# A graph network's prologue: first loads shared by two queues, and the second layer's weights folded during the first norm

## The chip, the cores and the metric

The kernel runs on one core of a Trainium2 chip. A core has TensorE (PE: matrix products and 128x128 transposes into PSUM), VectorE (DVE), ScalarE (ACT), GpSimd (POOL) and SyncE (SP), which here only issues transfers. Each engine runs its own list of instructions in order, and waits on semaphores for the others. Transfers are issued by SP and by POOL; 16 DMA engines carry them out. The metric is the device time of one execution in microseconds (us). Before the change its median is 2506.15 us over 4 runs (2505.47 to 2507.16).

## The reference

There are B = 16 graphs of N = 1024 nodes with D = 128 features, each with a dense adjacency of 1024 x 1024, all in float32. Two blocks follow each other, each with a residual and a layer norm:

```python
# block 0: one GNN layer
degree = adj.sum(-1)[:, :, None]
agg = einsum('bid,bij->bjd', x, adj) / degree
x = layernorm(x + relu(concat([x, agg], -1) @ W.T + b))
# block 1: four layers; layers 2 and 3 take earlier outputs beside the last one
src = nodes @ ws + bs;  dst = nodes @ wd + bd;  own = nodes @ wn + bn
src_agg = einsum('bjv,bij->biv', src, adj / row_norm)      # l2 norms of rows
dst_agg = einsum('bjv,bji->biv', dst, adj / column_norm)   # and of columns
out = tanh(concat([src_agg, own, dst_agg]) @ wu + bu)
x = layernorm(x + four_layers(x))
```

The kernel folds wu into ws, wd and wn once ("fold"), so that a layer is one product with a folded weight (message weights wm), one with the own weight (wown) and the two aggregations.

## The kernel before, in words

**Tiling.** A graph's adjacency lies in SBUF as eight blocks of 128 rows x 1024 columns (tile a), its nodes as eight blocks of 128 x 128 (xn). "Half" 1 is the latter four blocks or the latter 512 columns, half 0 the first. Columns sums of squares and row sums of squares give the norms; the transposed adjacency (at) is made by VectorE from rows loaded a second time (load_rows, in quarters q = 0 to 3), scaled by the inverse row norms (scale_rows) and transposed in blocks (transpose_rows).

**Batches.** A loop over b runs the four layers of graph b. While it does, the loads, norms and first GNN of graph b + 1 are woven into the layers' steps by hooks: a dictionary from a step's number to a function. For graph 0 nothing can be woven in, so a prologue (lines 718 to 909) does its loads, its first GNN and its norm, and layer 0 of graph 0 is a plain one (plain_layer) with its own hooks. The order of instructions on PE, DVE, ACT and POOL is the order in which the code writes them (line 712); SP's transfers follow program order too, each waiting until the one eight before it on its queue has landed.

**The prologue, step by step.**

- SP and POOL load w0, x and adjacency. A "pair" is two blocks of adjacency, 1 MB; SP loads two of its four row groups, POOL the other two. PAIRS goes through half 1 first. Then come b0 and the weights of the four layers (fetch_weights, eight small DMAs a layer), into a raw buffer that is the second adjacency buffer; rows of quarter 2 follow layer 0's weights, those of quarter 3 layer 1's.
- make_identity writes the identity that transposes on PE need; it is on POOL.
- to_xT, with_x and weights_of_x transpose x of a half, put x in the accumulator of the residual (yn) and start the product with W (pw).
- squares_of takes squares (ACT) and degrees (DVE) of a pair; gathers_of multiplies it with xn into pa (PE); add_square sums squares on POOL, into what becomes the column norms.
- degree_inverses, degree_row and scaled divide pa by the degree (agT); weights_of_agT ends pw and applies the relu (yT); with_y adds y to the residual; norm_stats and norm_write (or norm_write_act on ACT) are the layer norm; to_x1 transposes its result.
- fold_begin and fold_end fold one layer's weights: transposes of ws, wd, wn and products with the biases, then the products with wu. fold_end writes the folded weights to DRAM (wsave), from which message_weights fetches them.

**Buffers that decide an order.** The small PSUM tiles come from a pool of two (`small`), the larger ones from a pool of four (`product` without a number). A new tile waits until the oldest one in its pool has been read.

Of the kernel before, what the change touches and what calls it, by code (L numbers as in the profile page):

```python
# [9 lines left out]
AF = mybir.ActivationFunctionType  # L10
ALU = mybir.AluOpType
# [3 lines left out]
P = 128  # L15
NL = 4
CHUNKS = [1, 1, 2, 3]
G = 4
# [5 lines left out]
def adj_resnorm_kernel(ctx: ExitStack, tc: tile.TileContext, x, adj, w0, b0, layers, out):  # L24
# [113 lines left out]
            wm = flat[:, :(nch + 1) * 2 * P].rearrange("p (c v) -> p c v", c=nch + 1)  # L138
        return wr, wur, bc, wm, [raw.take(3 * P).rearrange("p (k v) -> p k v", k=3) for _ in range(nch)]

    def fold_begin(l, fetched, copy=nc.scalar.copy):

        wr, wur, bc, wm, wTs = fetched
        for c in range(CHUNKS[l]):
            pt = small(f"wtr{l}_{c}", [BPH, P])
            for k in range(3):
                nc.tensor.transpose(pt[:, k], wr[:, k, c], ident)
            copy(wTs[c], pt[:, :3])
        pm = small(f"bm{l}", [HW])
        for k in range(2):  # L150
            nc.tensor.matmul(pm[:, k * P:(k + 1) * P], bc[:, k:k + 1].to_broadcast([P, P]),
                             wur[:, PART[k]], start=True, stop=True)
        nc.tensor.matmul(pm[:, 2 * P:2 * P + 1], wur[:, PART[2]], bc[:, 2:3], start=True, stop=True)
        nc.scalar.copy(wm[:, 0], pm[:, :2 * P])
        nc.scalar.activation(bout[l], pm[:, 2 * P:2 * P + 1], AF.Identity, bias=bc[:, 3:4])

    def fold_end(l, fetched):
        _, wur, _, wm, wTs = fetched
# [571 lines left out]
    def load_nodes(h, q=nc.sync):  # L730
        for g in range(G):
            q.dma_start(xn[g * C:(g + 1) * C, h * BPH:(h + 1) * BPH], xv[h][g])

    nc.sync.dma_start(w0n, w0)
    for p, pair in enumerate(PAIRS):
        if p % 2 == 0:
            load_nodes(1 - p // 2)
        load_pair(nc.sync, pair, range(G // 2))
        load_pair(nc.gpsimd, pair, range(G // 2, G))
    make_identity(nc, ident)  # L740
    nc.sync.dma_start(b0c, b0.rearrange("(p o) -> p o", o=1))
    raw = Raw()
    wm = message_tile("wm1_0")
# [19 lines left out]
    def to_xT(h):  # L763
        pt = small(f"xtr0_{h}", [HW])
        for q in range(BPH):
            nc.tensor.transpose(pt[:, q * P:(q + 1) * P], xn[:, h * BPH + q], ident)
        nc.scalar.copy(nodes(xT[:, half(h)]), blocks(pt))
# [6 lines left out]
    sq = []  # L774
# [10 lines left out]
    def square(i):  # L785
        nc.scalar.activation(sq[i], a[:, i, :], AF.Square, accum_out=cols[:, i:i + 1])

    def add_square(i):
        nc.gpsimd.tensor_add(sq[4], sq[4], sq[i])

    def degree(i):
        nc.vector.reduce_sum(cols[:, 2 * NB + i:2 * NB + i + 1], a[:, i, :], axis=AX.X)

    def degree_inverses(h):
        s = slice(2 * NB + h * BPH, 2 * NB + (h + 1) * BPH)
        nc.vector.reciprocal(inv[:, s], cols[:, s])

    def gather(h, i):
        nc.tensor.matmul(pa[h], xn[:, i], a[:, i, half(h)], start=(i == BPH), stop=(i == BPH - 1))  # L799
# [18 lines left out]
    def degree_row(h):  # L818
        nc.scalar.copy(nodes(dinv[:, half(h)]), blocks(factor_bank(2, h, inv, f"dinv0_{h}")))

    def scaled(h):
        nc.vector.tensor_mul(agT[:, half(h)], pa[h], dinv[:, half(h)])

    def weights_of_x(h):
        pw[h] = product(f"pw0_0_{h}")
        nc.tensor.matmul(pw[h], w0T[:, 0], xT[:, half(h)], start=True, stop=False)

    def weights_of_agT(h):
        nc.tensor.matmul(pw[h], w0T[:, 1], agT[:, half(h)], start=False, stop=True)
        nc.scalar.activation(blocks(yT[:, half(h)]), nodes(pw[h]), AF.Relu, bias=b0c)  # L830

    def with_x(h):

        pn[h] = ps_t.tile([P, BPH, P], F32, tag="pt", name=f"yn0_{h}")
        nc.tensor.matmul(pn[h].rearrange("p q d -> p (q d)"), ident, xn[:, h * BPH:(h + 1) * BPH].rearrange("p q d -> p (q d)"),
                         start=True, stop=False)
# [9 lines left out]
            nc.tensor.transpose(pt[:, q * P:(q + 1) * P], x1n[:, h * BPH + q], ident)  # L846
        nc.scalar.copy(x1T[:, half(h)], pt)
# [12 lines left out]
    weights_of_x(0)  # L860
    degree_inverses(1)
    degree_row(1)
    squares_of(*PAIRS[2])
# [1 line left out]
    add_square(0)  # L865
    add_square(1)
    first, second = 2, 3
    square(first)
    square(second)
    gather(1, first)  # L870
    gather(1, second)
    degree(first)
    degree(second)
    degree_inverses(0)
    degree_row(0)
    gather(0, first)
# [35 lines left out]
    for b in range(B):  # L912
# [306 lines left out]
```

## Time and profile before

| what | value |
|---|---|
| median of 4 runs | 2506.15 us |
| the profiled execution's own time | 2505.47 us |
| its span, first to last instruction | 2503.7 us |
| PE busy over the span | 2484.4 us |
| mean granted PE clock | 0.998 |
| first gather (pa) on PE | 12.10 us |
| first x1n of the norm on ACT | 36.49 us |
| first d product of layer 0 | 48.5 us |
| start of the load of graph 1's adjacency | 77.42 us |

Times in the trace count from the span's start. A float32 product appears as two passes (128x512: 0.43 us each at full clock), so sixteen passes are eight products. A pass's row in the list of instructions gives start and duration, and in brackets the idle time of its engine before it with what ended that; durations overlap, so for sums the distances from start to start, as the chain that ended last shows them, are used. "PEclk" is the share of full clock that PE was granted.

### The profile page before, as it was taken

The page shows a single profiled execution, that of the slowest core. Times are in us where ns is not written, and L with a number is a line of the kernel's source. Part 1 is how long each engine was busy: PE and PEld are TensorE (multiplying, and loading weights), DVE is VectorE, ACT ScalarE, POOL GpSimd, SP SyncE. Part 2 cuts the span into 40 slices and gives each one's busy share as a digit, 9 for nine tenths or more (in the row PEclk, how much of TensorE's full clock was granted, in tenths as well). Part 3 has the DMA queues.
Part 4 walks back from the last instruction along what each step waited for, and adds up shares of the span by engine and source line. Part 5 has one row for each costly group of instructions (what it writes and reads, how often), then busy time and mean ns, then how long its engine had stood idle before and what let it go on. Part 6 is the DMA issues. An engine that isn't in the chain of part 4 may idle for free.

```text
span 2503.7 us, 30302 instructions
## 1 busy us (share of the span) xinstructions
PE 2484.4 (99%) x11693; PEld 1059.8 (42%) x11693; DVE 1660.6 (66%) x2030; ACT 836.4 (33%) x1553; POOL 519.9 (21%) x217
## 2 busy tenths in 40 slices
PE   8999999999999999999999999999999999999998
PEld 4443344433444344453434434334443344433444
DVE  5858667585675757667576675766758567585643
ACT  5414333142331423324143241432414333142411
POOL 5401204112040121302113030130301203112000
PEclk9999999999999999999999999999999999999999
DMA  9417245271543715426163451634417254271410
GB/s 201 99 47 147 55 96 104 51 143 41 102 100 66 134 34 104 106 66 127 35 124 84 86 106 47 131 65 101 96 46 147 54 100 102 51 144 40 93 24 9
DMA packets 358735, 219.63 MB, mean 88 GB/s; under 512 B 148928, under 2 KB 329408, under 8 KB 358592
## 3 DMA queue, kind: packets, MB, share of 16 engines
q1 hardware_dynamic: 357184, 213.51, 42.0%
q0 software_dynamic: 1408, 4.20, 0.7%
q8 instruction: 92, 1.51, 0.3%
q14 instruction: 51, 0.42, 0.1%
HBM read 199.17 MB, written 18.46 MB: 87 GB/s over the span
## 4 chain that ended last, share of the span: by engine, by line
PE 89%; SPq 3%; DMA 3%; DVE 2%; issue 2%; ACT 2%; POOL 0%; POOLq 0%; DVEq 0%; ACTq 0%
PE m L691 35%; PE z L691 26%; PE pt L503 15%; PE pa L179 8%; SPq L231 2%; PE pw L179 2%; DMA a<-in_adj_dram 2%; DVE e L664 1%; DMA out_dram<-y 1%; PE pa L799 1%; PE d L554 1%; ACT sq L248 0%; ACT sq L245 0%; POOL acc L250 0%; DVE cols L247 0%
## 5 line engine op out<-in xcount | busy, mean ns | idle before, releaser
L378 POOL TENSOR_TENSOR rs<-ve,mhalf 128x32 f32<-128x32 f32 x30 | 162.8, 5427 | 1363.9 <-DVE ve L376 1363.9
L691 PE MATMUL m<-T,S 128*64 128x512 f32 x1008 | 395.9, 594 | 0.0
L691 PE MATMUL z<-at,t 128*64 128x512 f32 x1224 | 383.7, 592 | 0.0
L691 PE MATMUL m<-a,t 128*64 128x512 f32 x1008 | 366.7, 594 | 0.0
L691 PE MATMUL m<-Q,S 128*64 128x512 f32 x768 | 339.2, 593 | 0.0
L691 PE MATMUL m<-at,t 128*64 128x512 f32 x828 | 311.2, 592 | 0.0
L506 DVE TENSOR_TENSOR t<-pt,wm 128x512 f32<-128x512 f32 x256 | 175.4, 690 | 169.5 <-PE pt L503 169.4
L252 POOL TENSOR_TENSOR acc<-acc,sq 128x1024 f32<-128x1024 f32 x90 | 220.6, 2451 | 138.9 <-ACT sq L248 135.3
L691 PE MATMUL z<-a,S 128*64 128x512 f32 x504 | 228.3, 593 | 0.0
L691 PE MATMUL z<-T,t 128*64 128x512 f32 x504 | 226.8, 592 | 0.0
L691 PE MATMUL z<-a,t 128*64 128x512 f32 x504 | 226.8, 592 | 0.0
L336 DVE TENSOR_TENSOR a<-a,cinv 128x512 f32<-128x512 f32 x250 | 157.8, 700 | 96.1 <-DMA cinv<-dr 92.8
L457 ACT ACTIVATE a<-a,rinv 128x256 f32<-128x256 f32 x480 | 198.2, 495 | 55.1 <-DMA a<-in_adj_dram 45.1
L503 PE MATMUL pt<-wm,f1T 128*128 128x256 f32 x768 | 213.8, 384 | 0.1
L179 PE MATMUL pa<-a,xn 128*64 128x512 f32 x960 | 208.7, 592 | 0.0
L691 PE MATMUL z<-at,S 128*64 128x512 f32 x444 | 202.6, 593 | 0.0
L691 PEld LDWEIGHTS m<-Q,S 128*64 128x64 f32 x768 | 104.1, 137 | 208.0 <-issue 206.1
L591 ACT COPY e<-m 64x512 f32<-64x512 f32 x63 | 36.6, 581 | 447.4 <-PE m L691 447.1
L691 PEld LDWEIGHTS m<-T,S 128*64 128x64 f32 x1008 | 117.8, 137 | 159.8 <-issue 158.7
L691 PE MATMUL z<-Q,t 128*64 128x512 f32 x384 | 172.6, 592 | 0.0
L691 PEld LDWEIGHTS z<-at,t 128*64 128x64 f32 x1224 | 120.8, 137 | 120.4 <-issue 111.3
L691 PEld LDWEIGHTS m<-a,t 128*64 128x64 f32 x1008 | 110.0, 137 | 125.7 <-issue 120.1
(197 smaller groups left out, 3783.8 us busy)
## 6 DMA issues: line engine op xcount, KB each, us to landing
a<-in_adj_dram SPq DMA_DIRECT2D x120, 512.0 KB, 12.8
a<-in_adj_dram SPq DMA_DIRECT2D x480, 128.0 KB, 4.1
xn<-in_x_dram SPq DMA_DIRECT2D x128, 64.0 KB, 2.0
wm<-wsave SPq DMA_DIRECT2D x16, 512.0 KB, 3.9
wm<-wsave SPq DMA_DIRECT2D x31, 256.0 KB, 3.1
xs<-in_x_dram SPq DMA_DIRECT2D x60, 128.0 KB, 3.5
cinv<-dr SPq DMA_DIRECT2D x30, 256.0 KB, 5.2
dinv<-dr SPq DMA_DIRECT2D x30, 256.0 KB, 5.0
```

Of the source, the lines that this page charges most:

```text
L179: nc.tensor.matmul(out[s], x[:, s], y, start=start, stop=stop)
L231: nc.sync.dma_start(ov[g, :, ks], ys[g * C:(g + 1) * C, ks])
L252: nc.gpsimd.tensor_add(acc, acc, sq)
L336: engine.tensor_mul(a[:, i, s], a[:, i, s], cinv[:, s])
L378: nc.gpsimd.tensor_tensor(rstd, ve, mhalf[:, :n], ALU.pow)
L457: nc.scalar.activation(st[:, k], st[:, k], AF.Copy, scale=rinv[:, q * QB + k:q * QB + k + 1])
L503: nc.tensor.matmul(pt[:, q], f[:, i * P:(i + 1) * P], wm[:, 1 + c], start=(k == 0), stop=(k == nch - 1))
L506: nc.vector.tensor_add(t[j][:, o:o + 2].rearrange("p k a v c -> p k (a v c)"), pt, wm[:, 0][:, None, :].to_broadcast([P, 2, 2 * P]))
L554: nc.tensor.matmul(nodes(o) if len(y.shape) == 4 else o, x_, y, start=start, stop=stop)
L591: nc.scalar.copy(e0[high], A[high])
L664: nc.vector.tensor_add(e0[high], e0[high], e1[high])
L691: nc.tensor.matmul(o, x, y, start=start, stop=stop)
```

## The change

Five things change, all in the prologue and in layer 0 of graph 0.

- x of both halves is loaded ahead of all adjacency, and each of the two queues takes half of the row groups of x, as it does of adjacency. The identity is written after POOL's share of x and ahead of its adjacency.
- The x steps of both halves (to_xT, with_x, weights_of_x) stand ahead of all gathers.
- Layer 1's weights are loaded ahead of quarter 2's rows and layer 2's ahead of quarter 3's; quarters 0 and 1 go on SP after layer 3's weights instead of on POOL during the norm.
- The end of the first GNN is reordered: one of the degrees goes to ACT as a copy with a sum; half 1 is scaled and multiplied ahead of half 0's last gather; squares of blocks 2 and 3 come later; the row norms' inverse and the last add of squares stand after the statistics.
- Layer 1's weights are folded between the norm's steps, with one copy on DVE and its bias copies put off (biases), instead of by hooks of layer 0. The hooks move: the fold of layer 2 to steps 5 and 8, that of layer 3 to 9 and 12. The column sums' transpose goes from the norm to the messages (first_half0).

```diff
-    def fold_begin(l, fetched, copy=nc.scalar.copy):
+    def fold_begin(l, fetched, copy=nc.scalar.copy, later=False):
...
-        nc.scalar.copy(wm[:, 0], pm[:, :2 * P])
-        nc.scalar.activation(bout[l], pm[:, 2 * P:2 * P + 1], AF.Identity, bias=bc[:, 3:4])
+        def biases():
+            nc.scalar.copy(wm[:, 0], pm[:, :2 * P])
+            nc.scalar.activation(bout[l], pm[:, 2 * P:2 * P + 1], AF.Identity, bias=bc[:, 3:4])
+        return biases if later else biases()
...
-    for p, pair in enumerate(PAIRS):
-        if p % 2 == 0:
-            load_nodes(1 - p // 2)
-        load_pair(nc.sync, pair, range(G // 2))
-        load_pair(nc.gpsimd, pair, range(G // 2, G))
+    shares = ((nc.sync, range(G // 2)), (nc.gpsimd, range(G // 2, G)))
+    for h in (1, 0):
+        for q, groups in shares:
+            load_nodes(q, h, groups)
     make_identity(nc, ident)
+    for pair in PAIRS:
+        for q, groups in shares:
+            load_pair(q, pair, groups)
...
-    for l, q in enumerate((2, 3, None, None)):
+    for l, q in enumerate((None, 2, 3, None)):
         fetched.append(fetch_weights(raw, l, nc.sync, None if l else wm))
         if q is not None:
             rows[q] = load_rows(0, q, places[q])
+    for q in (0, 1):
+        rows[q] = load_rows(0, q, places[q])
...
-    to_xT(1)
-    with_x(1)
-    weights_of_x(1)
+    for h in (1, 0):
+        to_xT(h)
+        with_x(h)
+        weights_of_x(h)
...
-    to_xT(0)
-    with_x(0)
-    weights_of_x(0)
...
-    square(first)
-    square(second)
+    nc.scalar.activation(sq[second], a[:, second, :], AF.Copy, accum_out=cols[:, 2 * NB + second:2 * NB + second + 1])
+    degree(first)
     gather(1, first)
     gather(1, second)
-    degree(first)
-    degree(second)
     degree_inverses(0)
     degree_row(0)
+    scaled(1)
     gather(0, first)
+    weights_of_agT(1)
+    square(first)
+    square(second)
     gather(0, second)
-    scaled(1)
     add_square(first)
-    nc.vector.tensor_scalar_max(cols[:, :NB], cols[:, :NB], NORM_EPS * NORM_EPS)
-    nc.gpsimd.tensor_tensor(inv[:, :NB], cols[:, :NB], mhalf[:, :NB], ALU.pow)
-    add_square(second)
-    weights_of_agT(1)
+    with_y(1)
     scaled(0)
     weights_of_agT(0)
-    with_y(1)
-    with_y(0)
     stats = {1: norm_stats(pn[1], range(BPH), "0_0_1", True)}
     fold_begin(0, fetched[0])
+    with_y(0)
     fold_end(0, fetched[0])
     stats[0] = norm_stats(pn[0], range(BPH), "0_0_0")
+    root_inverses(cols, inv, slice(NB))
+    add_square(second)
+    biases = fold_begin(1, fetched[1], nc.vector.tensor_copy, True)
     for q in range(BPH):
         norm_write_act(x1n[:, BPH + q], pn[1][:, q], stats[1], q)
-    for q in (0, 1):
-        rows[q] = load_rows(0, q, places[q], nc.gpsimd)
-    acct = column_transpose(0, st0)
     to_x1(1)
+    biases()
+    fold_end(1, fetched[1])
...
-                column_reduce(0, st0, acct)
+                column_sums(0, st0)
...
-            hooks = {1: lambda *_: inverses(0, st0, NB), 3: rows0, 4: folded(1, fold_begin), 6: folded(1, fold_end),
-                     7: cinv0, 9: lambda *_: fold_and_scale(2, 0), 11: second0, 12: folded(2, fold_end),
-                     14: lambda *_: fold_and_scale(3, 1), 18: first0, 20: folded(3, fold_end), 26: sums0}
+            hooks = {2: lambda *_: inverses(0, st0, NB), 3: rows0, 5: folded(2, fold_begin), 7: cinv0,
+                     8: folded(2, fold_end), 9: lambda *_: fold_and_scale(3, 0), 11: second0, 12: folded(3, fold_end),
+                     14: lambda *_: scale_rows(rows[1], 1, rinv), 18: first0, 26: sums0}
```

More of the change, by code (lines that the diff above doesn't have):

```diff
@@ L728, in load_pair, with load_nodes @@
             q.dma_start(a[g * C:(g + 1) * C, h * BPH + k:h * BPH + k + 2], av[h][g, :, k:k + 2])
-    def load_nodes(h, q=nc.sync):
-        for g in range(G):
+    def load_nodes(q, h, groups):
+        for g in groups:
             q.dma_start(xn[g * C:(g + 1) * C, h * BPH:(h + 1) * BPH], xv[h][g])
     nc.sync.dma_start(w0n, w0)
-    for p, pair in enumerate(PAIRS):
-        if p % 2 == 0:
-            load_nodes(1 - p // 2)
-        load_pair(nc.sync, pair, range(G // 2))
-        load_pair(nc.gpsimd, pair, range(G // 2, G))
+    shares = ((nc.sync, range(G // 2)), (nc.gpsimd, range(G // 2, G)))
+    for h in (1, 0):
+        for q, groups in shares:
+            load_nodes(q, h, groups)
     make_identity(nc, ident)
+    for pair in PAIRS:
+        for q, groups in shares:
+            load_pair(q, pair, groups)
     nc.sync.dma_start(b0c, b0.rearrange("(p o) -> p o", o=1))
@@ L867, in adj_resnorm_kernel @@
     first, second = 2, 3
+    nc.scalar.activation(sq[second], a[:, second, :], AF.Copy, accum_out=cols[:, 2 * NB + second:2 * NB + second + 1])
+    degree(first)
+    gather(1, first)
+    gather(1, second)
+    degree_inverses(0)
+    degree_row(0)
+    scaled(1)
+    gather(0, first)
+    weights_of_agT(1)
     square(first)
     square(second)
-    gather(1, first)
-    gather(1, second)
-    degree(first)
-    degree(second)
-    degree_inverses(0)
-    degree_row(0)
-    gather(0, first)
     gather(0, second)
-    scaled(1)
     add_square(first)
-    nc.vector.tensor_scalar_max(cols[:, :NB], cols[:, :NB], NORM_EPS * NORM_EPS)
-    nc.gpsimd.tensor_tensor(inv[:, :NB], cols[:, :NB], mhalf[:, :NB], ALU.pow)
-    add_square(second)
-    weights_of_agT(1)
+    with_y(1)
     scaled(0)
     weights_of_agT(0)
-    with_y(1)
-    with_y(0)
     stats = {1: norm_stats(pn[1], range(BPH), "0_0_1", True)}
     fold_begin(0, fetched[0])
+    with_y(0)
     fold_end(0, fetched[0])
     stats[0] = norm_stats(pn[0], range(BPH), "0_0_0")
+    root_inverses(cols, inv, slice(NB))
+    add_square(second)
+    biases = fold_begin(1, fetched[1], nc.vector.tensor_copy, True)
     for q in range(BPH):
         norm_write_act(x1n[:, BPH + q], pn[1][:, q], stats[1], q)
-    for q in (0, 1):
-        rows[q] = load_rows(0, q, places[q], nc.gpsimd)
-    acct = column_transpose(0, st0)
     to_x1(1)
+    biases()
+    fold_end(1, fetched[1])
     for q in range(BPH):
```

## The prediction

> **What bounds the kernel now.** I read the page's first part, then the stretches of 20 us, then TensorE's instructions in order of time, and last the other engines where TensorE stands.
>
> The page's first part: engines with their busy time.
>
> ```profile
> PE 2484.4 (99%) x11693; PEld 1059.8 (42%) x11693; DVE 1660.6 (66%) x2030; ACT 836.4 (33%) x1553; POOL 519.9 (21%) x217
> ```
>
> TensorE (PE) leaves 2503.7 - 2484.4 = 19.3 us idle in all. The busy time by stretch (start and end, length, then PE, PEld, DVE, ACT, POOL, granted clock, DMA share, GB/s) says where:
>
> ```profile
> 0.00:20.00 20.00, 12.34 (x31) 5.84 (x32) 6.92 (x12) 6.76 (x12) 8.21 (x17) 1.00 0.94 231
> 20.00:40.00 20.00, 17.39 (x69) 9.86 (x68) 13.79 (x32) 10.79 (x23) 16.84 (x13) 0.95 0.91 180
> 40.00:60.00 20.00, 19.57 (x83) 12.65 (x83) 11.92 (x19) 11.59 (x30) 9.00 (x14) 0.88 1.02 204
> 100.00:120.00 20.00, 20.00 (x94) 8.55 (x91) 18.41 (x15) 12.79 (x23) 15.40 (x5) 1.00 0.01 4
> ```
>
> 7.66 + 2.61 + 0.43 = 10.7 us of it lie in the first 60 us, where also the clock falls below 1.00. From 100 us on PE is full, so time is won or lost only in the prologue of batch 0. PE there, in order of time (start, duration, instruction, in brackets the idle time before and its releaser):
>
> ```profile
> 7.68 1.08 PE L766 MATMUL xtr<-ident,xn 128*128 128x128 f32 x4 [0.65 <-DMA xn<-in_x_dram]
> 12.10 7.28 PE L799 MATMUL pa<-a,xn 128*128 128x512 f32 x16 [0.66 <-DMA a<-in_adj_dram]
> 19.22 0.60 PE L766 MATMUL xtr<-ident,xn 128*128 128x128 f32 x4
> 19.66 1.02 PE L835 MATMUL yn<-xn,ident 128*128 128x512 f32 x2
> 20.52 1.10 PE L826 MATMUL pw<-x_T,w0T 128*128 128x512 f32 x2
> 37.00 1.52 PE L846 MATMUL x1tr<-ident,x1n 128*128 128x128 f32 x4 [1.89 <-ACT x1n L412]
> 39.20 2.07 PE L503 MATMUL pt<-wm,x_T 128*128 128x256 f32 x4 [0.67 <-ACT x_T L847]
> 42.67 3.84 PE L503 MATMUL pt<-wm,x_T 128*128 128x256 f32 x12
> ```
>
> Three things: PE waits until 12.10 for adjacency; the other half's x work (19.22 to 21.6) is done after it; at 35.1 to 39.2 PE waits for the first norm. The norm's own chain, all engines in order of time:
>
> ```profile
> 32.70 2.34 POOL L789 TENSOR_TENSOR sq<-sq,sq 128x1024 f32<-128x1024 f32 x1
> 34.02 1.05 DVE L395 TENSOR_SCALAR ve<-mv 128x4 f32<-128x4 f32 x1
> 35.15 1.02 POOL L401 TENSOR_TENSOR rs<-ve,mhalf 128x4 f32<-128x4 f32 x1
> 36.79 0.17 DVE L395 TENSOR_SCALAR ve<-mv 128x4 f32<-128x4 f32 x1
> ```
>
> The same ve takes 0.17 us alone and 1.05 us while POOL adds; it ends as POOL's add ends (35.04). And the clock by stretches of 2 us:
>
> ```profile
> 36.00:38.00 2.00, 0.96 (x3) 0.42 (x3) 1.86 (x6) 1.50 (x4) 1.34 (x3) 0.97 0.81 210
> 38.00:40.00 2.00, 1.33 (x4) 0.90 (x4) 1.50 (x5) 0.58 (x1) 2.00 (x5) 0.50 1.09 233
> 44.00:46.00 2.00, 2.00 (x9) 1.67 (x9) 1.10 (x3) 2.00 (x6) 1.56 (x3) 0.83 1.12 217
> ```
>
> After the norm's wait PE runs at half clock from about 37.9 to 44.7 us; work of about 5.3 us in it costs half of that, 2.65 us, too much.
>
> **What the Trainium skill says.** "TensorE: Matmul & The Clock Gate", Part 1: the array falls to half clock after an idle window of about 3.4 us and returns after a busy one, and the windows run free of the kernel. The trace agrees with 6.7 us of half clock, about two windows. "SBUF — State Buffer", Who interferes with whom: VectorE and GpSimd hold a shared port pair exclusively when VectorE works in a two-port mode or has two SBUF inputs; the loser waits for the whole instruction. 1.05 against 0.17 us agrees. "DMA: Bandwidth & Descriptors", Queues, rings and completion order: an engine takes turns between queues by packets. In the trace POOL's adjacency runs beside x: 2.6 MB have moved by 12.0 us (sum of GB/s over stretches of 1 us), while the first adjacency pair with its x and w0 is 1.4 MB.
>
> **The change, part by part.**
>
> *Loads.* Before, SP issues w0, x of half 1, two adjacency pairs (its half of the rows), x of half 0, two pairs; POOL issues all its adjacency from 1.34 us and writes the identity at 6.29. After, each queue issues its share of all x (4 DMAs each), POOL then the identity, then adjacency. POOL: 1.34 + 4 x 0.53 (its adjacency issues; x rows are shorter, 0.58 is the price of its row loads) = 3.5 to 3.7, identity 0.58 more (5.71 to 6.29): 4.1 to 4.3, 2 us sooner. Its adjacency starts 2.8 us later, and SP's first pair has the same bytes ahead on its ring (0.38 MB), but much less beside it. Up to the first pair 1.66 MB have to move in all; at the 230 GB/s of the first microseconds and then 300, estimated from those stretches, they have at about 9.3 us; I take 9 to 10 instead of 12.0, and each further 1.05 MB 3.5 us more: 13, 16.5, 20.
>
> PE: x of half 1 should land at about 5.0 (earliest landing after issue: 2.0 us). From x to the end of its pw took 3.76 us (7.68 to 11.44), the other half's three steps 0.44 + 0.86 + 0.94 = 2.24 from the chain. So gathers start at 11.0, or 12.3 if the array stays cold one window longer; I take 11.5. Then 16 gather passes, 6.9 us: the dinv transposes start at 18.4 instead of 21.62. Gain 3.2: 2.2 from x work in what was idle, 1.0 from x itself. Without the cover (adjacency at 12.0 still) it is 2.2.
>
> *Order of the first GNN's end.* The squares of blocks 2 and 3 go behind yT, scaled(1) and its weights ahead of gather(0, 3), one degree moves from DVE (1.21 us) to ACT (1.04 + 0.19). PE from 18.4: dinv 0.44, 12 passes 5.15, dinv 0.44, gather 0.86, weights 0.86, gather 0.86, ends 27.1; yT of half 1 is ready at 27.0, with_y(1) ends 27.5. DVE has scaled(0) (0.69) first; the statistics start at 28.0 instead of 32.27. They take 1.6 as before; POOL's add of block 2 starts when its square is done (28.2) and holds the port until 30.5, so ve still waits. But the add of block 3 no longer stands ahead of rs on POOL. rs, sh: x1n starts at 32.1 instead of 36.49. Gain 4.4. Moving the squares behind yT(1) puts yT(0) behind them on ACT: 29.3, so with_y(0) and the second half's statistics wait for it, and those are not the next thing needed.
>
> *Second layer's fold in the norm.* wtr, bm, wm of layer 1 leave the first layer, where they take 0.89 + 0.67 = 1.56 us between d steps, and fill 31 to 34 us, where PE would stand. The copy on DVE costs 0.5 ahead of norm_write; bias copies and wm's copies on ACT 1.2 between the two x1T copies, hidden under rp. Gain 1.56. Weights arrive in time: their 8 DMAs are issued ahead of the rows, from about 20 us.
>
> *What is late next.* add_square(3) follows inv on POOL (35.4 to 37.8). sp on DVE has two SBUF inputs and stands behind it until 37.8; rp on PE waits for sp, and pt behind rp (0.19 us of wait before, about 1.6 now). The transpose and the sum of acc (1.25 + 1.21) are now on DVE between rinv and the next t, so d starts at about 41.7 instead of 48.66: 7.0 sooner. Had PE kept its clock before, that would be 4.4; so 2.65 of the 7.0 is half clock that is not paid again.
>
> *Rows.* Rows of quarters 0 and 1 (16 DMAs) go from POOL's queue to the end of SP's loads: 16 x 0.5 = 8 us more of SP, in front of the wsave and kept writes, which nothing needs before about 77 us. POOL is free, and inv of the columns, which stood behind those issues at 51.47, comes at once. SP's order puts 8 more weight DMAs ahead of quarter 3's rows: issued from about 32 to 36.6, landing about 40.5 as before, while ACT wants them 3.25 us after rinv, at 41. Layer 2's fold on PE has its copies behind those scalings on ACT: a wait of 0.5, up to one for each us that the rows are later. The wsave3 that frees the raw buffer comes 10 us sooner, so the load of batch 1 does too; it was not on PE's path.
>
> Sum: 7.0 + 1.56 - 0.5 = 8.1 with the clock kept, 5.4 with it lost again. PE's work between 30 and 34 us is estimated from the above at 60% against 29% before (1.0 of 3.4 us); at 80% at half clock it did not rise. I take about even, slightly for kept, and 7.1 us as the forecast: 2505.47 - 7.1 = 2498.4 for the profiled execution, 2499.0 against the median of 2506.15 (the profiled one lies 0.7 below it).
>
> **Rivals.** *Clock lost again and a cold start*: gathers at 12.3, half clock after the norm; 5.4 - 0.8 = 4.6, at 2501.5. For it: the drop before, and transposes and waits still fill 32 to 38. Chance 0.24. *Adjacency sets the pace*: POOL's later issue makes the pairs land no earlier than before, PE waits at each, and only 1.56 and the reordered norm's 1.2 remain: about 2503.4. Against it: DMA is at 0.9 to 1.0 busy throughout, and the order wastes less. Chance 0.12. *Slower*: rows of quarter 3 on SP behind the weights. ACT cannot copy layer 2's folded weights before they are scaled; past 41 us each us costs one, so it eats the gain when they land at 49 and is 0.2% slower at 54. Against it: SP issued a DMA each 0.5 us without long waits. 2512 if so; chance 0.04.
>
> **Numbers.** 0.2% is 5.0 us, about what a measurement of this kernel can tell from no change. Likeliest case 0.60, between 2496 and 2501. The range takes in the first rival and most of the second: 2495.5 to 2503.5. Faster: 0.60 + half of the first rival + 0.02 = 0.74; slower 0.04; within 0.22.
>
> **What would show it.** Right: identity and w0tr near 4.2 us; gathers from 11 to 12.3 without DMA waits; x1n near 32; layer 1's wtr beside it; sp about 1.3 us long or late; d steps from about 42; clock 1.00 there. Wrong if gathers wait for a, if the clock is 0.50 for more than two windows, or if ACT waits for Q's rows before its second scaling.

## The result, and the profile after

The changed kernel takes 2502.39 us (median of 38 runs, 2499.47 to 2504.66). The kernel before, timed beside it, takes 2506.94 us (58 runs). The ratio is 0.9982 with a 95% interval of 0.9977 to 0.9986, so the change gains about 4.6 us. The forecast was a gain of 7.1 us. The profiled execution took 2502.88 us, with a span of 2501.1 us.

The first part of the page after, engines with their busy time:

```profile
PE 2483.9 (99%) x11693; PEld 1047.2 (42%) x11693; DVE 1656.7 (66%) x2030; ACT 836.3 (33%) x1554; POOL 512.3 (20%) x205
```

TensorE now leaves 17.2 us idle instead of 19.3. The stretches of 20 us after (columns as before):

```profile
0.00:20.00 20.00, 14.20 (x34) 6.80 (x34) 6.73 (x11) 7.20 (x12) 9.73 (x20) 1.00 0.90 241
20.00:40.00 20.00, 17.99 (x88) 11.34 (x86) 13.02 (x35) 12.53 (x29) 15.59 (x9) 1.00 0.83 166
40.00:60.00 20.00, 19.33 (x87) 12.76 (x88) 12.28 (x18) 12.05 (x32) 1.65 (x1) 0.91 1.08 213
```

TensorE is busier in the first 40 us. GpSimd has nearly nothing left between 40 and 60 us: 1.65 us instead of 9.00. TensorE's instructions after, in order of time:

```profile
4.85 1.06 PE L774 MATMUL xtr<-ident,xn 128*128 128x128 f32 x4
...
13.39 7.11 PE L807 MATMUL pa<-a,xn 128*128 128x512 f32 x16 [1.44 <-issue]
20.34 0.62 PE L285 MATMUL dinv<-ident,inv 128*128 128x128 f32 x4
...
35.02 1.05 PE L854 MATMUL x1tr<-ident,x1n 128*128 128x128 f32 x4
...
40.19 0.31 PE L183 MATMUL rp<-sp,fold 128*64 128x32 f32 x4 [1.88 <-DVE sp L307]
40.43 4.54 PE L507 MATMUL pt<-wm,x_T 128*128 128x256 f32 x12
46.85 2.84 PE L558 MATMUL d<-a,t 128*128 128x512 f32 x6
```

x is transposed 2.8 us sooner (4.85 for 7.68), yet the first gather starts 1.3 us later (13.39 for 12.10). Its idle time is put down to nothing in particular, but ACT's first square and DVE's first degree both start at 13.38, released by the adjacency. Since the other half's x steps are now behind TensorE by then, dinv still comes 1.1 us sooner (20.34 for 21.45 in this list; the 21.62 of the prediction is from the chain, which counts starts otherwise). The 1.89 us wait ahead of x1tr has gone. In its place is a wait of 1.88 us ahead of rp, whose cause stands among all engines in order of time:

```profile
34.82 0.17 DVE L399 TENSOR_SCALAR ve<-mv 128x4 f32<-128x4 f32 x1
...
37.65 2.34 POOL L797 TENSOR_TENSOR sq<-sq,sq 128x1024 f32<-128x1024 f32 x1
...
38.59 1.45 DVE L307 TENSOR_TENSOR sp<-inv,group 128x32 f32<-128x32 f32 x1
```

sp is 32 elements wide. It starts while GpSimd adds, and ends when the add ends, at 40.0. The clock after, by stretches of 2 us:

```profile
38.00:40.00 2.00, 0.31 (x3) 0.07 (x1) 2.00 (x2) 0.59 (x1) 1.99 (x1) 1.00 0.90 228
40.00:42.00 2.00, 1.81 (x8) 1.52 (x9) 1.47 (x4) 1.24 (x4) 0.00 (x0) 0.68 1.14 186
42.00:44.00 2.00, 2.00 (x6) 1.59 (x5) 1.75 (x3) 2.00 (x7) 0.00 (x0) 0.50 1.21 277
44.00:46.00 2.00, 2.00 (x7) 1.22 (x7) 1.37 (x2) 2.00 (x7) 0.00 (x0) 0.96 0.65 137
```

A stretch of 2 us at a mean clock c holds 2 x (1 - c) / 0.5 us of half clock. That makes 1.28 + 2 + 0.16 = 3.4 us here, from 40.7 to 44.2 us; before it was 6.8 us.

**The mark used below.** TensorE's work from the first d of layer 0 to layer 1's first product is nearly gapless, so the start of that product shows what the prologue gained. Before:

```profile
21.45 0.60 PE L281 MATMUL dinv<-ident,inv 128*128 128x128 f32 x4
...
48.50 1.88 PE L554 MATMUL d<-a,t 128*128 128x512 f32 x4
...
86.13 4.03 PE L503 MATMUL pt<-wm,f1T 128*128 128x256 f32 x16
```

After:

```profile
83.16 4.03 PE L507 MATMUL pt<-wm,f1T 128*128 128x256 f32 x16
```

From there to the end of the span the fourteen profiled executions took 2417.6 to 2420.8 us, in no clear order by kernel; the execution before, with 2417.6, is the shortest. Most of the scatter, in five of them, is a sum of waits of at most 0.9 us (pt for the tanh that writes f23T), 1.9 us in all in the execution after and 4.3 in another. So a span of one execution is good to about 1.5 us. The mark is better, but it too moves between executions of one kernel, by half a microsecond with the landing of the loads and by more with the clock, and the times of many runs decide.

### The profile page after: what moved, and what is told of

It is laid out like the page before. It is cut to its first block, busy times and chain, and to the rows that moved or that the text cites. A ratio compares the mean times of both kernels' runs of the same rounds, so it can differ in the third digit from the quotient of the medians.

```text
span 2501.1 us, 30299 instructions
## 1 busy us (share of the span) xinstructions
PE 2483.9 (99%) x11693; PEld 1047.2 (42%) x11693; DVE 1656.7 (66%) x2030; ACT 836.3 (33%) x1554; POOL 512.3 (20%) x205
## 4 chain that ended last, share of the span: by engine, by line
PE 84%; SPq 4%; DMA 4%; DVE 3%; issue 3%; ACT 2%; POOL 0%; POOLq 0%; DVEq 0%; ACTq 0%
PE m L695 34%; PE z L695 25%; PE pt L507 14%; PE pa L183 8%; SPq L235 3%; PE pw L183 2%; DMA a<-in_adj_dram 2%; DVE e L668 1%; DMA out_dram<-y 1%; ACT sq L252 1%; DMA raw<-in_L_gnn_ws_dram 1%; ACT sq L249 1%; POOL acc L254 0%; SPq L456 0%; DVE cols L251 0%
```

## The experiments

All ratios are to the kernel before on the same chip, with 95% intervals; one thousandth is 2.5 us. The other columns are from the one profiled execution of each kernel: the start of dinv's transposes, the time from there to the first d, the time from d to layer 1's first product, and the start of that product, all in us.

| kernel | ratio | dinv | dinv to d | d to layer 1 | layer 1 |
|---|---|---|---|---|---|
| before | 1 | 21.5 | 27.1 | 37.6 | 86.13 |
| the change | 0.9982 (0.9977 to 0.9986) | 20.3 | 26.5 | 36.3 | 83.16 |
| the change, second time | 0.9979 (0.9971 to 0.9987) | 19.8 | 24.8 | 36.3 | 80.98 |
| loads and x steps alone | 0.9991 (0.9983 to 0.9999) | 20.0 | 26.7 | 37.6 | 84.30 |
| change without these | 0.9987 (0.9981 to 0.9994) | 21.9 | 24.8 | 36.3 | 83.06 |
| fold alone | 1.0002 (0.9994 to 1.001) | 22.3 | 24.9 | 40.8 | 87.94 |
| rows 0 and 1 on SP alone | 1.0000 (0.9992 to 1.0009) | 22.7 | 27.0 | 37.6 | 87.30 |
| fold and these rows | 0.9985 (0.9979 to 0.9992) | 22.2 | 24.9 | 36.0 | 82.99 |
| change, these rows on GpSimd | 0.9992 (0.9986 to 0.9999) | 19.8 | 26.5 | 37.8 | 84.12 |
| change, sp on GpSimd | 0.9973 (0.9962 to 0.9985) | 20.6 | 22.9 | 36.9 | 80.34 |
| change, gap filled | 0.9984 (0.9977 to 0.9990) | 20.2 | 26.3 | 36.3 | 82.78 |
| change, more of x on SP | 0.9983 (0.9977 to 0.9990) | 19.8 | 24.8 | 36.3 | 80.97 |
| change, more adjacency on SP | 0.9976 (0.9967 to 0.9985) | 20.0 | 25.2 | 36.8 | 81.92 |
| three together | 0.9964 (0.9950 to 0.9978) | 18.5 | 22.9 | 36.3 | 77.66 |

The loads decide the first column, the first norm with its clock and sp the second, the fold and the column norms the third. The five executions with the old loads have dinv at 21.5 to 22.7 (mean 22.1), the six with the new ones, two pieces on each queue throughout, at 19.8 to 20.6 (mean 20.1). So the loads are worth 2.0 us there, with the first gather 0.6 later on the mean (13.1 against 12.5); the profile of before is an early one of its kind.

### Which part gains: loads, or the rest

Two kernels split the change. The first is the kernel before with the new loads and the x steps in front:

```diff
-    for p, pair in enumerate(PAIRS):
-        if p % 2 == 0:
-            load_nodes(1 - p // 2)
-        load_pair(nc.sync, pair, range(G // 2))
-        load_pair(nc.gpsimd, pair, range(G // 2, G))
+    shares = ((nc.sync, range(G // 2)), (nc.gpsimd, range(G // 2, G)))
+    for h in (1, 0):
+        for q, groups in shares:
+            load_nodes(q, h, groups)
     make_identity(nc, ident)
+    for pair in PAIRS:
+        for q, groups in shares:
+            load_pair(q, pair, groups)
...
-    to_xT(1)
-    with_x(1)
-    weights_of_x(1)
+    for h in (1, 0):
+        to_xT(h)
+        with_x(h)
+        weights_of_x(h)
...
-    to_xT(0)
-    with_x(0)
-    weights_of_x(0)
...
```

The second is the change with exactly that undone.

> The kernel before with the loads of the changed kernel alone (x of both halves first on two queues, identity sooner, the x steps of both halves ahead of the gathers). Theory (the loads help a little: gathers begin later, near 13.4 us, but the x work is already done): dinv starts about 1.3 us sooner than 21.62, and the time falls by about 1.3 us, ratio 0.9995. Rival (POOL's late half of the first pair eats the whole gain): first gather at 14 or later, no gain, ratio 1.0000 or above.

> The changed kernel with the loads and the x steps put back as they were before; all else as changed. Theory: 1.3 us slower than the changed kernel, so about 3.2 us faster than before, ratio 0.9987; first gather near 12.1. Rival (loads bring nothing): as fast as the changed kernel, ratio 0.9982. If the loads cost time, ratio below 0.9982.

Loads alone: 2506.03 us (13 runs) against 2508.20, 0.9991. The first gather is at 13.05, dinv at 19.99 instead of 21.45: 1.5 us sooner. Without the loads the change takes 2504.73 us (21 runs), 0.9987, with gathers at 12.45 and dinv at 21.92. So about 2 us of the gain belong to the loads and about 3.3 to the rest. Their sum, 5.5, lies within what the intervals allow for the whole; taking the loads out of the change costs only 1.3 by the ratios. The gathers come later with the new loads, and the gain is the x work of the other half that no longer stands between them and dinv (9.35 us from the one to the other before, 6.95 after). The order of the loads, their split over two queues and the place of the x steps were not tried apart.

### The fold of layer 1 and the rows on GpSimd's queue

The fold in the norm was given 1.56 us in the prediction. It was tried alone, on the kernel before:

```diff
...
+    biases = fold_begin(1, fetched[1], nc.vector.tensor_copy, True)
     for q in range(BPH):
         norm_write_act(x1n[:, BPH + q], pn[1][:, q], stats[1], q)
...
+    biases()
+    fold_end(1, fetched[1])
...
-            hooks = {1: lambda *_: inverses(0, st0, NB), 3: rows0, 4: folded(1, fold_begin), 6: folded(1, fold_end),
+            hooks = {1: lambda *_: inverses(0, st0, NB), 3: rows0,
```

> The kernel before with the fold of layer 1 alone moved between the steps of the norm, and taken out of layer 0's hooks. Theory (TensorE stood there anyway): 1.56 us of TensorE work leave the layer and nothing is added, ratio 0.9994. Rival (the fold's copies on ScalarE and VectorE delay x1T and norm_write by 0.5 to 1.2 us, and the wait only moves): 0 to 0.5 us, ratio 0.9998 to 1.0000.

It gained nothing: 2508.15 us against 2508.20. TensorE's wait ahead of x1tr fell from 1.89 to 0.45 us, and d started 1.3 us sooner (47.16), but then came this, TensorE first:

```profile
54.53 1.95 PE L285 MATMUL cinvp<-ident,inv 128*128 128x128 f32 x8 [2.93 <-POOL inv L302]
56.28 2.74 PE L558 MATMUL d<-a,t 128*128 128x512 f32 x4
```

and GpSimd of the same kernel:

```profile
50.42 1.30 POOL L456 DMA_DIRECT2D rows<-in_adj_dram  x2 [1.06 <-DMA Q<-in_adj_dram]
52.22 0.58 POOL L456 DMA_DIRECT2D rows<-in_adj_dram  x1 [0.49 <-DMA Q<-in_adj_dram]
52.81 1.67 POOL L302 TENSOR_TENSOR inv<-cols,mhalf 128x8 f32<-128x8 f32 x1
```

GpSimd issues the 16 row loads from 38.84, and from the ninth on they wait for an earlier load to land (the brackets). The power that makes inv stands behind the last, at 52.81. TensorE, now early, has nothing else and waits 2.93 us, after which cinvp's passes take nearly twice and the first d steps one and a half times as long as before (1.04 and 1.88 us): the clock is at 0.65 and 0.50 from 54 to 58 us. In the kernel before inv was as late, to 53.14, but TensorE came to cinvp only at 54.46:

```profile
51.47 1.67 POOL L298 TENSOR_TENSOR inv<-cols,mhalf 128x8 f32<-128x8 f32 x1
```

```profile
54.46 1.04 PE L281 MATMUL cinvp<-ident,inv 128*128 128x128 f32 x8
```

The late power was hidden by the very work that the fold takes away.

If so, the fold must pay once those rows go to SP, the rows alone must pay nothing, and putting them back must cost the change about half its gain. Fold and rows:

```diff
             rows[q] = load_rows(0, q, places[q])
+    for q in (0, 1):
+        rows[q] = load_rows(0, q, places[q])
...
-    for q in (0, 1):
-        rows[q] = load_rows(0, q, places[q], nc.gpsimd)
```

> The kernel before with layer 1's weights folded in the norm (as in the run of that alone) and the rows of quarters 0 and 1 issued on SP's queue after the last weights, in place of GpSimd's. Theory (the fold alone gained nothing because the power of the column norms stood behind GpSimd's issue of those rows): the 2.93 us wait at cinvp is gone, layer 1's first product starts 1.0 to 2.0 us sooner than the 87.94 of the fold alone, and the kernel is 1.0 to 2.0 us faster than before, 0.9992 to 0.9996. Rival (the fold doesn't pay wherever the rows are issued, as the PE work is only moved): 0.9998 to 1.0002.

The rows alone are this last diff on the kernel before; in the third kernel the change gets `load_rows(0, q, places[q], nc.gpsimd)` back, ahead of biases.

> The kernel before with the rows of quarters 0 and 1 issued on SP's queue after the last weights and nothing else. Theory (each of fold and rows is worth nothing without the other: with layer 1's fold still among the products of layer 0, TensorE comes to cinvp at 54.46 in any case): 0.9996 to 1.0003, and layer 1's first product at 85.5 to 86.5. Rival (the rows alone were the gain, 3.9 us with the fold, and the fold is worth nothing): 0.9983 to 0.9988.

> The changed kernel with the rows of quarters 0 and 1 back on GpSimd's queue, at the end of the norm as before. Theory (what makes the fold pay is that these issues no longer stand ahead of the power of the column norms): that power starts at 52 us or later in place of about 48, cinvp waits 2 to 4 us, and 2 to 3 us of the gain are lost: 0.9990 to 0.9995. Rival (SP's queue or GpSimd's, it is the same): 0.9980 to 0.9984.

Fold and rows on SP: 2504.33 us (21 runs), 0.9985, a gain of 3.9 us, more than was expected. The table has it as 2.2 us less than before from dinv to d and 1.7 less from d to layer 1. GpSimd, and then TensorE, of that kernel:

```profile
46.90 1.64 POOL L302 TENSOR_TENSOR inv<-cols,mhalf 128x8 f32<-128x8 f32 x1 [8.14 <-DVE cols L301]
```

```profile
51.32 1.04 PE L285 MATMUL cinvp<-ident,inv 128*128 128x128 f32 x8
```

inv follows its own input now, 5.9 us sooner than with the fold alone, and cinvp comes 3.2 us sooner with no wait. Rows alone: 2507.84 us against 2507.93, nothing; layer 1's product is later there than was said (87.30), but only because the adjacency and with it dinv came late in that execution, and the two stages behind dinv are those of before. The change with the rows back on GpSimd: 2506.30, 0.9992, so 3.7 us more than the change beside it (2502.57). GpSimd and TensorE there:

```profile
52.26 1.67 POOL L302 TENSOR_TENSOR inv<-cols,mhalf 128x8 f32<-128x8 f32 x1
```

```profile
53.98 1.09 PE L285 MATMUL cinvp<-ident,inv 128*128 128x128 f32 x8 [1.24 <-POOL inv L302]
```

The wait is 1.24 us, shorter than the expected 2 to 4, partly because this execution had lost clock before (0.54 and 0.60 from 40 to 44 us) and came late to cinvp. From d to layer 1 it takes 1.5 us more than the change (37.8 against 36.3); the other 1.7 us by which this execution is behind the change's second is that loss of clock, which the change has in its first too. So the times show a loss of 3.7 us, and the profile accounts for less than half of it by the rows. That neither part gains alone and both together do is shown; together they are the larger part of the change.

Fold and rows alone (0.9985) do as well as the change without its loads (0.9987), which has all the reordering of the first GNN's end besides. Both take 24.8 to 24.9 us from dinv to d: the time that the reordering wins goes into the wait for sp, which is 1.88 us there and 0.60 in the kernel with fold and rows alone. The 2.2 us that both have won against before are near the 2.65 that the prediction estimated for the half clock, and neither lost the clock in the norm; but no profile has the old norm with the clock kept, so this share of the clock is argued and not measured.

### The stall ahead of rp, and the clock

sp was put on GpSimd, ahead of the last add of squares:

```diff
-    def row_inverses(b, inv):
+    def row_inverses(b, inv, engine=nc.vector):
...
-        nc.vector.tensor_mul(spread, inv[:, :NB].rearrange("p (h k) -> p h k", h=NH)[:, :, None, :]
+        engine.tensor_mul(spread, inv[:, :NB].rearrange("p (h k) -> p h k", h=NH)[:, :, None, :]
...
     root_inverses(cols, inv, slice(NB))
+    spread0 = row_inverses(0, inv, nc.gpsimd)
     add_square(second)
...
-                rinv = gather_inverses(0, row_inverses(0, inv))
+                rinv = gather_inverses(0, spread0)
```

> The changed kernel with the product sp computed on GpSimd, right after inv and ahead of the last add of squares, instead of on VectorE, where it stood behind that add for 1.45 us. Theory (the wait of rp for sp is on TensorE's path): rp starts near 38.3 instead of 40.19, TensorE's clock stays at 1.00 or falls later, and the kernel is 1.9 to 3.7 us faster than the changed one, ratio 0.9975 to 0.9968 to the kernel before. Rival (d waits for the transpose and sum of acc on VectorE, which wait for the same add, so the stall only moves behind rp): less than 1 us, ratio 0.9979 or above.

2501.17 us (6 runs), 0.9973. All engines of that kernel in order of time:

```profile
38.00 0.24 POOL L307 TENSOR_TENSOR sp<-inv,group 128x32 f32<-128x32 f32 x1
38.20 2.36 POOL L797 TENSOR_TENSOR sq<-sq,sq 128x1024 f32<-128x1024 f32 x1
38.48 0.31 PE L183 MATMUL rp<-sp,fold 128*64 128x32 f32 x4
```

sp takes 0.24 us, rp waits for nothing, and the clock is 1.00 throughout. From dinv to d it is 22.9 us, 1.9 less than the change takes with the clock kept. What is late next: the transpose of acct on DVE waits 1.56 us for the add, which TensorE doesn't feel, and ACT:

```profile
44.06 3.30 ACT L461 ACTIVATE Q<-Q,rinv 128x256 f32<-128x256 f32 x8 [1.69 <-DMA raw<-in_L_gnn_wd_dram]
```

The wait is named after a weight load, but the instruction reads Q. SP issued quarter 3's rows until 39.65, behind the weights of layer 2, and its loads take about 4 us to land. TensorE pays 0.81 us of it at layer 2's bm, and from d to layer 1 the kernel takes 0.6 us more than the change.

The ratio of 0.9973 is about 2.3 us below the change's, with intervals that overlap, and holds two things, the stall of 1.88 us and the clock. To part them, the stall was left and filled with matmuls of no use, whose result nothing reads:

```diff
                 to_x1(0)
+                filler = product("filler", 0)
+                for _ in range(4):
+                    nc.tensor.matmul(filler, ident, x1n[:, :BPH].rearrange("p q d -> p (q d)"), start=True, stop=True)
                 rinv = gather_inverses(0, row_inverses(0, inv))
```

> The changed kernel with four 128x512 matmuls of no use, about 1.8 us, on TensorE in the stall before rp; they write a bank that is not in use then, and nothing reads them. Theory that the clock is what the stall costs most (in the change's profile the clock is at half from 40.7 to 44.2 us, after the idle 1.88 us before rp): with the gap filled the clock stays at 1.00 and the kernel is 1.0 to 1.8 us faster than the change, 0.9975 to 0.9978 of before. Rival (the gain of 2.5 us from spreading on GpSimd was the stall itself, and the drop of the clock is not set by this gap): the time of the change within 0.5 us, 0.9980 to 0.9984, with or without the drop.

2504.35 us, 0.9984: no gain, but the filler was sized wrongly:

```profile
37.96 3.60 PE L933 MATMUL filler<-x1n,ident 128*128 128x512 f32 x8
41.49 0.31 PE L183 MATMUL rp<-sp,fold 128*64 128x32 f32 x4
```

Each of the four products is two passes, 3.5 us in all, so rp came 1.3 us later than in the change. The time is the rival's, and the clock stayed at 1.00; but since the filler itself costs more than the stall, the time leaves the price of the clock open. The change run a second time answers better.

> The changed kernel as it is, once more, for comparison on the same chip as the three beside it. Theory: 0.9980 to 0.9984 of before; if the half clock of its first profile (40.7 to 44.2 us) belongs to that execution and not to the kernel, the clock is at 1.00 from 36 to 50 us here and the first d starts at 45.0 to 45.4 in place of 46.85. Rival (the 1.88 us stall before rp always costs the clock): half clock again between 40 and 45, d at 46.5 or later.

2502.57 us (14 runs), 0.9979. TensorE, and then the stretches of TensorE alone (busy, clock, DMA share, GB/s):

```profile
12.83 7.11 PE L807 MATMUL pa<-a,xn 128*128 128x512 f32 x16 [1.80 <-issue]
...
39.69 0.31 PE L183 MATMUL rp<-sp,fold 128*64 128x32 f32 x4 [1.87 <-DVE sp L307]
...
44.67 2.84 PE L558 MATMUL d<-a,t 128*128 128x512 f32 x6
```

```profile
40.00:42.00 2.00, 2.00 (x10) 1.00 1.16 200
42.00:44.00 2.00, 2.00 (x8) 1.00 1.20 270
```

The same stall, and no half clock. From rp to d it is 4.98 us here and 6.66 in the first execution: the half clock costs 1.7 us where it falls. Of the six profiled executions with this stall (the change twice, without its loads, the two of the next section, rows back on GpSimd) two lost the clock after it, for 3.4 us both times. The kernel before, loads alone and rows alone, with the idle norm, lost it in each of their three profiles, for 6.8 us each. The four with a filled gap, a short one or none (filled, fold with rows, sp on GpSimd, three together) kept it; the fold alone kept it too until its wait of 2.93 us at cinvp, and then lost it for 3.4 us. The lengths, 3.4 and twice 3.4, agree with the window of about 3.4 us in the Trainium skill's "TensorE: Matmul & The Clock Gate", Part 1. That less idle time makes the drop rarer or shorter fits this count, which is small, and a larger one: the mean clock of each execution is known to a thousandth. It is 0.998 or less in 96 of 169 executions of the three kernels with the idle norm, and in 12 of some 190 of all the others.

### Why the first pair of adjacency is late

The prediction had it land at 9 to 10 us; it came at 13.4. The queues of the change between 5 and 7 us (queue: packets, MB, share; q1 is SP's, q0 GpSimd's):

```profile
q1 hardware_dynamic: 116, 0.37, 86.4%
q0 software_dynamic: 32, 0.07, 11.0%
```

SP is mostly through with its x by then and moves adjacency (3 KB a packet on average). GpSimd still has x: with the 0.02 and 0.17 MB that its queue moved in the four microseconds before, these 0.07 MB make up its 0.26 MB of x, and its eighth adjacency issue waits for x until 8.24 us. Two ways out: more of x on SP, so that GpSimd comes to its adjacency sooner, or more of the first adjacency on SP.

```diff
-        for q, groups in shares:
+        for q, groups in ((nc.sync, range(3)), (nc.gpsimd, range(3, G))):
             load_nodes(q, h, groups)
```

```diff
-    for pair in PAIRS:
-        for q, groups in shares:
+    for p, pair in enumerate(PAIRS):
+        s = 3 if p < 2 else 1
+        for q, groups in ((nc.sync, range(s)), (nc.gpsimd, range(s, G))):
             load_pair(q, pair, groups)
```

> The changed kernel with three of each half's four pieces of x on SP's queue and one on GpSimd's, in place of two and two; the adjacency stays two and two. Theory (GpSimd's share of the first pair of adjacency rows lands last because two pieces of x stand ahead of it on that queue): the first gather starts at 10.5 to 12.0 us in place of 13.39, dinv's transposes 1.2 to 2.5 sooner than 20.34, and the kernel is 1.5 to 2.5 us faster than the change, 0.9972 to 0.9978 of before. Rival (all transfers share the same rate, and it is the sum of the bytes that is late): the first gather stays at 13.0 or later, ratio 0.9982.

> The changed kernel with x two and two as the change has it, but three of four pieces of the first two adjacency pairs on SP's queue and one on GpSimd's, and one and three for the last two pairs. Theory (SP's queue moved 0.29 to 0.37 MB in each 2 us while GpSimd's moved 0.02 to 0.17, so GpSimd's piece is the late one): the first gather at 10.5 to 11.5 us, dinv's transposes at 17.8 to 18.8, the whole 1.5 to 2.5 us faster than the change, 0.9972 to 0.9978 of before. Rival (the sum of the bytes decides): first gather 13.0 or later, ratio 0.9982. A second rival: the gathers start sooner but the later pairs, now mostly on GpSimd's queue, land late, and the gain is given back before the scaled gather at 26.15.

More of x on SP: 2504.13 us, 0.9983, first gather at 12.89, no better than the change. Its queues between 5 and 7 us:

```profile
q0 software_dynamic: 105, 0.36, 78.3%
q1 hardware_dynamic: 148, 0.07, 19.4%
```

The picture is turned round. Now SP has x left, in packets of about 0.5 KB, and GpSimd adjacency. Neither queue is slow by itself: the one that still carries x moves a fifth of what the one with adjacency does. So this was the wrong cure, and the cause named in its theory (GpSimd's share is late) is only half of it. Its rival, that the sum of the bytes decides, falls with the next run, which has the same bytes and its first gather at 11.7.

More adjacency on SP: 2501.96 us (11 runs), 0.9976. TensorE there:

```profile
11.74 3.70 PE L808 MATMUL pa<-a,xn 128*128 128x512 f32 x8
16.25 3.67 PE L808 MATMUL pa<-a,xn 128*128 128x512 f32 x8 [0.81 <-DMA a<-in_adj_dram]
```

The first pair is there at 11.7 us, but the second, also three quarters on SP, comes at 16.2 and TensorE waits again: dinv is at 19.95, where the change's two profiles have 20.34 and 19.83. So the second rival holds in what it says of the gain (what the first pair wins, the second gives back), not in its reason, since the late pair is also mostly on SP; which piece of it landed last stays open. The ratio of 0.9976 is in the theory's range, but its step is not: dinv was to be at 17.8 to 18.8. The ratio is lower than the change's 0.9982 and 0.9979, but the intervals overlap, and the trace shows no gain at dinv that would make it more.

### Three together

From the landings above, three quarters of the first pair and half of the others should suit both. With that, sp on GpSimd and quarter 3's rows ahead of layer 2's weights:

```diff
+        s = 2 if p else 3
+        for q, groups in ((nc.sync, range(s)), (nc.gpsimd, range(s, G))):
...
-    for l, q in enumerate((None, 2, 3, None)):
+    for l, qs in enumerate(((), (2, 3), (), ())):
...
-        if q is not None:
+        for q in qs:
             rows[q] = load_rows(0, q, places[q])
...
```

> The changed kernel with three things at once: sp on GpSimd ahead of its last sum of squares (as in the run of that alone); three of four pieces of the first adjacency pair on SP's queue and two of four of the others; quarter 3's rows issued straight after quarter 2's, ahead of the last two layers' weights. Theory, worked from the runs so far: SP's pieces land at about 7.8, 9.0 and 10.2 us and GpSimd's at 11.7, 13.4 and 15.0, so the first pair is there at 11.7 and the second at 15.0, when TensorE has just finished the first at 15.4; dinv's transposes at 18.6 to 19.0 in place of 20.34; no wait at rp; no wait of 0.8 us at the second layer's bm; layer 1's first product at 77.7 to 79.0 in place of 80.34 with sp alone; the kernel 8 to 9.5 us faster than before, 0.9962 to 0.9968. Rival (the gains do not add, since the pairs behind the first come later and the rest is given back): 0.9970 to 0.9976, as with sp alone.

```profile
11.61 7.03 PE L808 MATMUL pa<-a,xn 128*128 128x512 f32 x16
18.48 0.60 PE L285 MATMUL dinv<-ident,inv 128*128 128x128 f32 x4
...
36.38 0.31 PE L183 MATMUL rp<-sp,fold 128*64 128x32 f32 x4
...
41.36 2.84 PE L558 MATMUL d<-a,t 128*128 128x512 f32 x6
```

These are TensorE's instructions in that kernel. The gathers run through without a wait, dinv is 1.9 us sooner than in the change's first profile, rp waits for nothing, ACT scales both quarters without a wait and bm's wait is 0.24 us. It takes 2499.03 us (5 runs, 2497.96 to 2499.90), 0.9964, about 8.9 us faster than before and 3.5 faster than the change beside it. All five runs are below all fourteen of the change beside it. The table divides the gain over the change's second execution: 1.4 us at dinv, by the first pair, and 1.9 from dinv to d, by sp. From d to layer 1 it takes what the change takes, so the earlier rows of quarter 3 win back the 0.6 us that sp alone gave up; they were not tried by themselves.

## Why the prediction was right or wrong

**Direction and kind: right, the size less than said.** The gain that the profiles show lies in the first 87 us, as was said from the stretches of time. Of the forecast 7.1 us, 4.6 came. The time of 2502.39 us lies in the stated range but outside the likeliest case, 2496 to 2501. That the first rival named just 4.6 us is luck: it takes off 2.65 for a lost clock, which the change kept in one of its two profiles, and 0.8 for late gathers, while the terms that were short are the two below, the loads and the way from sp to d.

**Loads: the step that failed.** The identity came at 4.31 us (said: 4.1 to 4.3) and x's steps ran in time that had been idle, as said. But "I take 9 to 10" for the first pair was 13.4 (12.8 the second time). The sum took the total of bytes at the total rate, as if the two queues came through at the same time. The rate was right: by 9 us 1.64 MB had moved, of the 1.66 that the sum needs by 9.3. But they were not the bytes of the first pair: the queue with x lags, and the other fills the time with bytes of later pairs, which nobody waits for yet. So the gathers waited for adjacency, which the prediction had named as a sign of being wrong. The gain at dinv was 2.0 us between the means of the profiles (1.1 and 1.6 for the change's two against the one before) instead of 3.2. The rival "adjacency sets the pace" had this wait, of 1.4 to 1.8 us at the first gather, but was wrong that little else would remain.

**Order of the first GNN's end: right in size, and worth nothing at d.** From the first gather to x1n it was to be 20.6 us and was 20.8 (13.39 to 34.17). But the kernel with fold and rows in the old order takes the same 24.9 us from dinv to d as the change takes with the clock kept (24.8), because sp is what is waited for next.

**What is late next: right in kind, one term too small.** The stall of sp behind the add of squares was foreseen with "about 1.6" and measured 1.88. From the end of sp (37.8) to d (41.7) 3.9 us were allowed, for the transpose and the sum of acc on DVE between rinv and t. TensorE sets this step: 12 passes of pt take 2.7 us, z 1.8, rp and pc 0.5, and the trace shows 4.98, so 1.1 more. Added to 41.7 with the late gathers (1.3 and 1.9) that makes 44.1, and with 1.7 of half clock 46.4; d started at 44.67 and 46.85.

**Fold: the size right, its condition missed.** From the first d to layer 1's first product it was 86.13 - 48.50 = 37.6 us before and 83.16 - 46.85 = 36.3 after, 1.3 less, where 1.56 - 0.5 was said. But the prediction put the rows' move down as work for SP with "inv ... comes at once" and gave it no price. Without it the fold gains nothing, and with the rows back the change loses 3.7 us. The lines that say so were in the profile of before: inv at 51.47, cinvp at 54.46, the lateness of the first hidden only by the work ahead of the second.

**The clock: not contradicted.** "About even" that it is lost again: two of six profiles, one of the change's own two, too few to tell even odds from others. Where it fell, it fell after the stall for sp and for 3.4 us, not after the norm for 6.8.

**The sum.** Said was 8.1 us with the clock kept. The mark shows 86.13 - 80.98 = 5.15 in the execution that kept it, and 2.97 in the one that didn't; the times show 4.6 and 5.4. d is sooner by 3.8 (48.50 to 44.67) instead of 7.0, and the 1.3 behind it is as said.

## What to carry to other kernels

When work is taken out of a stretch, look at what else was late behind it: a value that arrives just in time is a wait as soon as its reader comes sooner. An engine that both issues loads and computes in one order, as GpSimd does here, holds its computation back by every issue that waits for an earlier load. And when two queues share one tile, balance what each must land by the first use, not the bytes in all: here the queue that still had x was slow beside the one with adjacency.

## What the runs showed that was not expected

- Loads of x (512-byte rows) move 0.07 MB in 2 us beside adjacency on the other queue, which moves 0.36 to 0.37 in the same time, whichever of the two queues carries x. Why the share is so uneven was not settled, nor whether the length of the rows has to do with it; the number of packets does not explain both cases (32 against 116, and 148 against 105).
- A stall of the same 1.9 us cost the clock in two executions and not in four others of nearly the same kernel; where it did, the half clock lasted 3.4 us, and 6.8 us after the idle norm.
- From the ninth of its 16 row loads on, GpSimd's issue waits for earlier loads, up to 2.0 us for one. SP's issue in the change does so too: after 8 adjacency loads its next were 1.1 to 2.1 us apart until 19 us (b0c at 7.79, then the weights at 9.02, 10.11, 12.10, 13.71, 15.34, 16.94 and 19.06).
